# Layer 0 of a four-layer network: the two depthwise convolutions, the norms and the input transposes placed anew in the strip cycle

## The chip, the cores and the metric

The kernel runs on one core of a Trainium2 chip. TensorE (PE) multiplies matrices and transposes, VectorE (DVE) works elementwise and reduces, ScalarE (ACT) evaluates activation functions, GpSimd (POOL) works elementwise, and SyncE (SP) issues most DMAs. Each engine takes its instructions in its own program order and waits on semaphores for the others. The metric is the device time of one execution in microseconds (us); lower is better.

## The reference, cut to what matters

The network has four layers; the change touches layer 0. Its input is eight images of 64 x 64 positions with 192 channels, in fp32. With the shapes left out, layer 0 computes for every image:

```python
def layer0(x):
    x0 = group_norm(x)                      # statistics over a whole image
    x1 = x0 + dwconv3x3(x0, cpe1)           # first depthwise convolution
    h  = layernorm(x1, ln1)
    z, xBC, dt = in_proj(h)                 # 384, 512 and 6 columns
    xBC = silu(causal_conv1d(xBC, 4 taps))
    dt  = softplus(dt + dt_bias)
    y   = ssd(xBC, dt, A) + D * x_part      # chunked scan over the 4096 positions
    y   = rms_norm(y * silu(z)) @ out_proj
    x2  = x1 + y
    x2  = x2 + dwconv3x3(x2, cpe2)          # second depthwise convolution
    h2  = layernorm(x2, ln2)
    x3  = x2 + fc2(gelu(fc1(h2)))           # 192 -> 768 -> 192
    return x + x3                           # and statistics of it for layer 1
```

Layer 1 is a four-directional selective scan; layers 2 and 3 are two further 3x3 depthwise convolutions. They come after layer 0 and are the same in both kernels.

## The kernel before, in words

**Strips and cycles.** Channels lie on partitions as 2 x 96. Each image is cut into 8 strips of 512 positions (8 rows of 64), so there are 64 strips. One turn of the main loop (L700-711) is a cycle; in cycle q every stage of the layer works on its own strip: a strip takes several cycles from its input to its output, and the stages of different strips share a cycle. Inside the cycle the main stage, the scan, works on strip q.

**Who sets the order.** Layer 0 is inside `with every_engine(tc)`: the order of the instructions on PE, DVE, ACT and POOL is exactly the order in which the program emits them. Only SP, the DMA queue, is ordered by a scheduler. The stages are Python generators; each `yield` marks a place where another stage may put instructions. `together(...)` goes round its generators and takes one step of each in turn until all are done; a generator named twice in it makes two steps a round, and one given as `beside` moves on only while the others last. `one_by_one(...)` chains generators. A `yield` more or less therefore moves instructions on all engines.

**The three phases of a cycle**, named by the activation table that ScalarE needs:

- *gelu*: `together(widen(q-3), one_by_one(project_xbc(q), project_out(q-1)), conv1(q+1), residual(q-3))`. `widen` (L643, gelu L647) is fc1. `project_xbc` (L399) makes the columns of xBC and runs the causal convolution on DVE. `project_out` transposes the gated result (L608), multiplies with out_proj (L615) and adds to the strip on DVE (L617). `conv1` is the first depthwise convolution: an affine step on ACT that applies the group norm (L322, two of them), then 16 taps on DVE (L304). `residual` adds on POOL (L661).
- *silu*: `exponents(q, 0, made)`, six ACT operations (L506) that prepare chunk 0, then `together(gates(q), beside=[second])`. `gates` multiplies the z columns (L424), and applies silu to them (L432) and to cv, the output of the causal convolution (L438 the last). `second` is `conv2(q-2)`, the second depthwise convolution. Then `exp_and_ln()` loads ACT's table for exp and ln.
- *chunks*: the strip is scanned in 4 chunks of 128 positions. `front` transposes cv (L524) and copies it out of PSUM on ACT (`xb`, L532), makes the score matrix, applies exp on ACT, prepares xdt, xw and xd on POOL (L538-540), multiplies M on DVE (L541) and issues the next chunk's `exponents`. `back` multiplies with the carried state (L563, L565), updates it on DVE (L571, by the product of L565), and adds the chunk's outputs in one bank (L574, L576); DVE (L585, L586) gates them. Beside them run `narrow(q-3)` (fc2: 12 matmul pairs L677, then L680 on DVE adds the residual, and POOL issues the DMA to x1d), and `norms`, a chain of four: `norm1(q+1)` (layer norm: transposes L344, statistics on DVE, rsqrt and scaling on ACT L357, transposes back L369), `steps(q+1)` (the step sizes: L449 on PE, then exp and ln on ACT, then the cumulative sums L477/478 on PE from dA), `norm2(q-2)` (which waits until `conv2` has emitted its last tap), and `take_in` for the image that comes next (loads x, transposes it at L249, copies it to DRAM in channel order, takes statistics; on the last strip of an image it makes the group norm's scale).

**Buffers that tie the stages.** [...] tp 2 (transposes and out_proj), mm 2 (project_xbc, gates, front, the step sizes), fc 1 (narrow), y 3 (widen, back). In SBUF, x0h and res have two buffers, csb three, xs five. The lines that the change turns on:

```python
def bank(tag):
    return mk(psum, [128, NJ], tag, bufs={"tp": 2, "mm": 2, "fc": 1, "y": 3}[tag])
...
def norm2(q):
    if at(q):
        while ("conv2", q) not in done:
            yield
```

Of the kernel before, what the change touches and what calls it, by code (L numbers as in the profile page):

```python
# [33 lines left out]
def mk(pool, shape, tag, **kw):  # L34
    Names.n += 1
    return pool.tile(shape, F32, tag=tag, name=f"{tag}_{Names.n}", **kw)
# [110 lines left out]
def together(*threads, beside=()):  # L147

    threads = list(threads)
    while threads:  # L150
        for t in list(threads) + list(beside):
            if next(t, threads) is threads and t in threads:
                threads.remove(t)
# [20 lines left out]
def layer0(ctx: ExitStack, tc, a, dr, x, x1, mv1, cst):  # L174
# [62 lines left out]
    def take_in(b, r):  # L237
        if b >= B:
            return
        if r == 0:  # L240
            st0[b] = mk(pool, [CP, CT, NCH, 6], "st0")
        xt = mk(pool, [128, NB, C], "xt", bufs=2)
        nc.sync.dma_start(xt, x[b].rearrange("(g j p) c -> g p j c", p=128, j=NB)[r])
        xc = mk(pool, [CP, CT, NJ], "xc", bufs=2)
        yield
        for ct in range(CT):
            ps = bank("tp")[:CP]
            for j in range(NB):
                nc.tensor.transpose(ps[:, j * 128 : (j + 1) * 128], xt[:, j, ct * CP : (ct + 1) * CP], ident)  # L249
            yield  # L250
            nc.scalar.copy(xc[:, ct, :], ps)
            nc.vector.bn_stats(st0[b][:, ct, r, :], ps)
            yield
        nc.sync.dma_start(x0[b][:, :, r * NJ : (r + 1) * NJ], xc)
        if r < NCH - 1:
            return
        mv, d, q = (mk(pool, s, t) for s, t in (([CP, CT, 2], "mv0"), ([CP, CT], "gd"), ([CP, CT], "gq")))
        gm, sc, nb = (mk(pool, [CP, CT], t, bufs=2) for t in ("gm", "sc0", "nb0"))
        for ct in range(CT):
            nc.vector.bn_aggr(mv[:, ct, :], st0[b][:, ct, :, :])  # L260
        yield
        ps = bank("tp")[:CP, 0:CT]
        nc.tensor.matmul(ps, grp, mv[:, :, 0], start=True, stop=True)
        yield
        nc.vector.tensor_copy(gm, ps)
        nc.vector.tensor_tensor(d, mv[:, :, 0], gm, ALU.subtract)
        nc.vector.tensor_tensor(q, d, d, ALU.mult)
        nc.vector.tensor_tensor(q, q, mv[:, :, 1], ALU.add)
        yield
        ps = bank("tp")[:CP, 0:CT]  # L270
        nc.tensor.matmul(ps, grp, q, start=True, stop=True)
        yield
        nc.vector.tensor_scalar(q, ps, EPS, None, ALU.add)
        rsqrt(nc, pool, q, sc, "gr")
        nc.vector.scalar_tensor_tensor(nb, gm, -1.0, sc, ALU.mult, ALU.mult)
        norm[b] = sc, nb
        yield

    def load_strip(q):

        if not at(q):
            return
        b, r = strips[q]
        t = x0h[q] = mk(pool, [CP, CT, HW], "x0h", bufs=2)
        lo, hi = max(0, r * R - 1), min(H, (r + 1) * R + 1)
        d0 = lo - (r * R - 1)
        nc.sync.dma_start(t[:, :, d0 * W : (d0 + hi - lo) * W], x0[b][:, :, lo * W : hi * W])
# [26 lines left out]
    def conv1(q):  # L314
        if not at(q):
            return
        b, r = strips[q]
        t = x0h.pop(q)
        sc, nb = norm[b]
        lo, hi = (W if r == 0 else 0), (HW - W if r == NCH - 1 else HW)  # L320
        for ct in range(CT):
            nc.scalar.activation(  # L322
                t[:, ct, lo:hi], t[:, ct, lo:hi], AF.Identity, bias=nb[:, ct : ct + 1], scale=sc[:, ct : ct + 1]
            )
        if r == 0:
            nc.gpsimd.memset(t[:, :, 0:W], 0.0)
        if r == NCH - 1:
            nc.gpsimd.memset(t[:, :, HW - W :], 0.0)
        v = xs[q] = mk(pool, [CP, CT, HW], "xs", bufs=5)
        yield  # L330
        yield from conv(t, v[:, :, W : W + NJ], c1w, mid[:, 0, :], c1b)

# [54 lines left out]
    def project_xbc(q):  # L387
        if not at(q):
            return
        raw = mk(pool, [128, 4, 3 + NJ], "raw")  # L390
        cv = cvs[q] = mk(pool, [128, 4, NJ], "cv")
        if strips[q][1] == 0:
            nc.gpsimd.memset(raw[:, :, 0:3], 0.0)
        else:
            nc.gpsimd.tensor_copy(raw[:, :, 0:3], halos.pop(q))
        for o in range(4):
            ps = bank("mm")
            for ct in range(CT):
                nc.tensor.matmul(  # L399
                    ps, w_xbc[:, ct, o * 128 : (o + 1) * 128], hn1[q][:, ct, :], start=ct == 0, stop=ct == CT - 1  # L400
                )
            yield
            nc.scalar.copy(raw[:, o, 3:], ps)  # L403
            yield
            nc.vector.tensor_scalar(
                cv[:, o, :], raw[:, o, 3:], cdw[:, o, 3:4], cdb[:, o : o + 1], ALU.mult, ALU.add
            )
            for k in range(3):
                nc.vector.scalar_tensor_tensor(
                    cv[:, o, :], raw[:, o, k : k + NJ], cdw[:, o, k : k + 1], cv[:, o, :], ALU.mult, ALU.add  # L410
                )
        halos[q + 1] = mk(pool, [128, 4, 3], "halo", bufs=2)
        nc.gpsimd.tensor_copy(halos[q + 1], raw[:, :, NJ : NJ + 3])  # L413
        yield
# [221 lines left out]
    def widen(q):  # L636
        if not at(q):
            return
        ff = ffs[q] = mk(pool, [128, 6, NJ], "ff")
        for o in range(6):  # L640
            ps = bank("y")
            for ct in range(CT):
                nc.tensor.matmul(  # L643
                    ps, f1w[:, ct, o * 128 : (o + 1) * 128], hn2[q][:, ct, :], start=ct == 0, stop=ct == CT - 1
                )
            yield
            nc.scalar.activation(ff[:, o, :], ps, AF.Gelu, bias=f1b[:, o : o + 1])  # L647
        del hn2[q]
        yield

    def load_residual(q):
        if at(q):
            b, r = strips[q]
            ress[q] = mk(pool, [CP, CT, NJ], "res", bufs=2)
            nc.sync.dma_start(ress[q], x0[b][:, :, r * NJ : (r + 1) * NJ])

    def residual(q):
        if at(q):
            x2 = x2s.pop(q)
            for ct in range(CT):  # L660
                nc.gpsimd.tensor_tensor(ress[q][:, ct, :], ress[q][:, ct, :], x2[:, ct, :], ALU.add)  # L661
            yield

    def narrow(q):
        if not at(q):
            return
        b, r = strips[q]
        sl = slice(r * NJ, (r + 1) * NJ)
        ff = ffs.pop(q)
        if r == 0:  # L670
            st1[b] = mk(pool, [CP, CT, NCH, 6], "st1", bufs=2)
        res = ress.pop(q)
        xo = mk(pool, [CP, CT, NJ], "xo")
        for ct in range(CT):
            ps = bank("fc")[:CP]
            for o in range(6):
                nc.tensor.matmul(ps, f2w[:, o, ct * CP : (ct + 1) * CP], ff[:, o, :], start=o == 0, stop=o == 5)  # L677
                if ct > 0 or o > 1:
                    yield
            nc.vector.scalar_tensor_tensor(xo[:, ct, :], ps, f2b[:, ct : ct + 1], res[:, ct, :], ALU.add, ALU.add)  # L680
            nc.vector.bn_stats(st1[b][:, ct, r, :], xo[:, ct, :])
        nc.gpsimd.dma_start(x1[b][:, :, sl], xo)
        if r == NCH - 1:
            for ct in range(CT):
                nc.vector.bn_aggr(mv1[:, b, ct, :], st1[b][:, ct, :, :])
        yield

    def one_by_one(*threads):
        for t in threads:
            yield from t  # L690
# [4 lines left out]
    with every_engine(tc):  # L695
        for r in range(NCH):
            if r == NCH - 1:
                exp_and_ln()
            together(take_in(0, r))
        load_strip(0)  # L700
        for q in range(-1, len(strips) + 3):
            load_strip(q + 2)
            load_residual(q - 2)
            together(
                widen(q - 3), one_by_one(project_xbc(q), project_out(q - 1)), conv1(q + 1), residual(q - 3)
            )
            made, second = {}, conv2(q - 2)
            exponents(q, 0, made)
            together(gates(q), beside=[second])
            exp_and_ln()  # L710
            norms = one_by_one(norm1(q + 1), steps(q + 1), norm2(q - 2), take_in(*divmod(q + NCH + 1, NCH)))
            together(front(q, made), norms, narrow(q - 3), back(q, made), norms, second)


@with_exitstack
# [596 lines left out]
```

## Time and profile before

| | us |
|---|---|
| median of 3 runs (26507.2 to 26526.69) | 26510.6 |
| the profiled execution's own time | 26508.04 |
| its span on the core (mean granted TensorE clock 0.942) | 26506.2 |
| layer 0 in it: from the start to the end of its drain | 5740 |
| undisturbed cycle of layer 0, from one first z silu (L432) to the next | 85.4 |

The first two differ by 2.6 us, so durations from the profile can be set beside the median. Layer 0 takes about a fifth of the span; the other four fifths belong to layers 1 to 3. Cycles are read as the distance of ScalarE's first L432 of a cycle to the next. Most are 85.36 to 85.8; the first are 78.67, 68.48, 95.45 and 91.0, some near image boundaries are 87 to 93, and the last full ones are 88.7.

In the cycle from 2999.90 to 3085.30, the groups with the most work, in calls x mean, are on PE L677 24 x 0.65 us, L643 24 x 0.60 and L399 16 x 0.59; on DVE the taps of the second convolution 16 x 0.88 and of the first 16 x 0.74. A DMA of each kind moves 384 KB a cycle (480 for x0h), and the DMA engines are at most partly busy in every slice. In the page, each digit of a row is a tenth of a fortieth of the span (PEclk: of full clock); in a list by stretches, columns are the stretch, its length, then busy us and instructions of each engine, then the granted clock, the DMA share and GB/s. In a list of waits a line names the engine and its waiting instruction, what released it, and total, number and longest wait in us.

### The profile page before, as it was taken

To read this page: it belongs to the slowest core of one execution; us is meant where nothing else is said; L and a number is where in the kernel's file an instruction comes from. 1 tells how busy PE (TensorE), PEld (TensorE's weight loads), DVE (VectorE), ACT (ScalarE), POOL (GpSimd) and SP (SyncE) were. 2 spreads that over 40 slices of the span, in tenths; PEclk is the share of its full clock that TensorE was granted. 3 is DMA by queue.
4 is the path that set the end of the run, shared out by engine and by line. 5 is a ranking of instruction groups with operands and counts; after the bars stand their busy time and mean duration, and the time that the engine had idled before them with its cause. 6 is when DMAs were issued, how large, how long until landed. Compare 5 with 4: busy or idle time off the path is not lost.

```text
span 26506.2 us, 442347 instructions
## 1 busy us (share of the span) xinstructions
PE 23817.3 (90%) x156160; PEld 18514.6 (70%) x156160; DVE 22196.4 (84%) x25001; ACT 20110.0 (76%) x40019; POOL 17618.6 (66%) x18396
## 2 busy tenths in 40 slices
PE   7888888887799999999999999999999999987766
PEld 4444444444478888888888888888888888863322
DVE  6777777655589999999999999999999999986566
ACT  4555555433379999999999999999999999984322
POOL 2222222210079999999999999999999999972100
PEclk8888888888899999999999999999999999998878
DMA  1111111112233333333333333333333333346411
GB/s 55 42 43 43 42 43 42 34 44 89 90 103 97 94 102 96 95 101 96 96 100 98 94 101 97 96 99 98 95 99 99 95 98 97 96 137 198 126 34 29
DMA packets 1461962, 2275.55 MB, mean 86 GB/s; under 512 B 247181, under 2 KB 773133, under 8 KB 1458202
## 3 DMA queue, kind: packets, MB, share of 16 engines
q1 hardware_dynamic: 1445402, 2196.90, 28.2%
q0 software_dynamic: 14336, 50.34, 0.5%
q8 instruction: 1232, 20.19, 0.3%
q14 instruction: 992, 8.13, 0.1%
HBM read 1811.37 MB, written 435.42 MB: 85 GB/s over the span
## 4 chain that ended last, share of the span: by engine, by line
PE 36%; ACT 29%; DVE 13%; POOL 13%; issue 6%; DMA 2%; POOLq 0%; SPq 0%; DVEq 0%; ACTq 0%
ACT dA L1039 12%; POOL hc L1089 10%; PE pd L1045 6%; ACT sb L1023 6%; PE yt L978 5%; DVE h L1080 5%; ACT bd L1023 4%; PE y L643 3%; PE fc L677 3%; DVE x L71 2%; DVE u L823 2%; PE mm L793 2%; DMA yin<-y 2%; PE pd L1047 2%; PE mm L399 2%
## 5 line engine op out<-in xcount | busy, mean ns | idle before, releaser
L1089 POOL TENSOR_TENSOR hc<-h,bc 128x512 f32<-128x512 f32 x12288 | 15425.9, 1289 | 488.7 <-DVE h L1080 342.0
L1080 DVE TENSOR_TENSOR_SCAN h<-dA,st,pd 128x512 f32<-128x512 f32 x10752 | 12949.9, 1263 | 530.9 <-PE pd L1045 369.4
L1039 ACT ACTIVATE dA<-dl,A_logs 128x512 f32<-128x512 f32 x12288 | 8787.0, 715 | 46.9 <-DVE h L1080 39.6
L978 PE MATMUL yt<-sq,hc 128*128 128x128 f32 x49152 | 7488.5, 275 | 198.8 <-POOL hc L1089 97.3
L1045 PE MATMUL pd<-bd,dut 128*128 128x128 f32 x49152 | 6582.1, 277 | 254.4 <-DVE h L1080 232.1
L1045 PEld LDWEIGHTS pd<-bd,dut 128*128 128x128 f32 x49152 | 5969.2, 192 | 610.3 <-PE yt L978 343.0
L978 PEld LDWEIGHTS yt<-sq,hc 128*128 128x128 f32 x49152 | 5668.1, 141 | 642.1 <-POOL hc L1089 623.3
L1023 ACT ACTIVATE sb<-dut,xt 128x384 f32<-128x384 f32 x8192 | 4763.5, 606 | 1.1 <-DVE dut L964 1.0
L1047 PE MATMUL pd<-sq,sb 128*128 128x128 f32 x24576 | 3739.5, 275 | 9.1 <-DVE h L1080 0.2
L1047 PEld LDWEIGHTS pd<-sq,sb 128*128 128x128 f32 x24576 | 2820.9, 141 | 480.6 <-DVE dl L951 380.8
L1023 ACT ACTIVATE bd<-sq,xt 128x128 f32<-128x128 f32 x8192 | 3011.1, 393 | 0.0
L1080 DVE TENSOR_TENSOR_SCAN h<-dA,pd 128x512 f32<-128x512 f32 x1536 | 1772.6, 1204 | 114.8 <-PE pd L1045 75.6
L71 DVE SCALAR_TENSOR_TENSOR x<-x,w,x 96x3969 f32<-96x3969 f32 (+1 forms) x192 | 838.3, 4366 | 488.6 <-ACT x L64 485.6
L538 POOL TENSOR_TENSOR xdt<-xb,dtv 128x384 f32<-128x384 f32 x256 | 220.7, 862 | 1365.5 <-ACT xb L532 1365.5
L800 POOL COPY xa<-xa 128x192 f32<-128x192 f32 x56 | 19.9, 356 | 1387.9 <-ACT xa L797 1387.9
L413 POOL COPY halo<-raw 128x12 f32<-128x12 f32 x64 | 12.8, 201 | 1380.8 <-ACT raw L403 1380.8
L304 DVE SCALAR_TENSOR_TENSOR x<-xs,cpe_w,x 96x504 f32<-96x504 f32 (+1 forms) x1024 | 899.4, 878 | 30.2 <-ACT x L292 20.4
L823 DVE SCALAR_TENSOR_TENSOR u<-xa,conv_w,u 128x504 f32<-128x504 f32 x1152 | 850.1, 743 | 63.5 <-ACT u L817 25.1
L937 PE MATMUL mm<-xs,w_dt 13*128 13x512 f32 x1536 | 863.0, 641 | 1.8 <-DVE dl L951 1.0
L677 PE MATMUL fc<-ff,fc_w 128*96 128x512 f32 x1536 | 858.9, 676 | 2.7 <-DVE xo L680 2.7
L1091 POOL COPY st<-h 128x3 f32<-128x3 f32 x4096 | 821.8, 201 | 0.0
L793 PE MATMUL mm<-g,w_in 96*128 96x512 f32 x768 | 487.5, 769 | 333.4 <-ACT g L739 332.9
(234 smaller groups left out, 26955.9 us busy)
## 6 DMA issues: line engine op xcount, KB each, us to landing
bc<-bcd SPq DMA_DIRECT2D x4096, 256.0 KB
yin<-y SPq DMA_DIRECT2D x256, 768.0 KB
csb<-csd SPq DMA_DIRECT2D x256, 384.0 KB
dut<-ut SPq DMA_DIRECT2D x128, 768.0 KB
y<-ys SPq DMA_DIRECT2D x128, 768.0 KB
dut<-ut SPq DMA_DIRECT2D x256, 384.0 KB
y<-ys SPq DMA_DIRECT2D x256, 384.0 KB
xt<-x1d SPq DMA_DIRECT2D x128, 384.0 KB
```

The source lines that it names most:

```text
L71: nc.vector.scalar_tensor_tensor(d[:, h0:h1, w0:w1], s[:, h0 + dy : h1 + dy, w0 + dx : w1 + dx], w[:, ct, tap : tap + 1], d[:, h0:h1, w0:w ...
L304: nc.vector.scalar_tensor_tensor(d[:, :, w0:w1], s[:, dy : dy + R, w0 + dx : w1 + dx], w[:, ct, tap : tap + 1], d[:, :, w0:w1], ALU.mult, ...
L677: nc.tensor.matmul(ps, f2w[:, o, ct * CP : (ct + 1) * CP], ff[:, o, :], start=o == 0, stop=o == 5)
L793: nc.tensor.matmul(ps, w_in[:, ct, o * 128 : (o + 1) * 128], g[:, ct, :], start=ct == 0, stop=ct == CT - 1)
L823: nc.vector.scalar_tensor_tensor(uv[:, o, :, w0:w1], tv[:, o, dy : dy + R, w0 + dx : w1 + dx], cw[:, o, tap : tap + 1], uv[:, o, :, w0:w1] ...
L978: nc.tensor.matmul(yt[:, t * 128 : (t + 1) * 128], src[:, t * 128 : (t + 1) * 128], mat, is_transpose=mat is ident, start=first and t == 0 ...
L1023: nc.scalar.activation(v, src, AF.Copy, scale=m["xt"][:, t, 1 + R1 + n : 2 + R1 + n])
L1039: nc.scalar.activation(dA, ready[s]["dl"][:, o, :], AF.Exp, scale=aneg[:, k, o, n : n + 1])
L1045: nc.tensor.matmul(dst, ready[s]["dut"][:, t, cols], brows[g, t], start=True, stop=True)
L1047: nc.tensor.transpose(dst, brows[g, t][:, cols], ident)
L1080: nc.vector.tensor_tensor_scan(h[:, o, rev], decay.pop(j)[:, rev], turned.pop(j)[:, rev], 0.0 if first else st[:, o, n : n + 1], ALU.mult, ...
L1089: nc.gpsimd.tensor_tensor(hc, h[:, o, :], held[g], ALU.mult)
```

## The change

It does five things in layer 0:

- `conv2` moves from the silu and chunk phases of one cycle to the gelu phase of the next, and `conv1` from the gelu phase to the chunk phase. Everything after conv2 (norm2, widen, residual, narrow) is one cycle later for its strip, so the loop has one more turn, and `xs` needs seven buffers instead of five. Before the loop the first strips' conv1 runs on its own.
- `norms` is now norm1, norm2, steps, statistics in this order.
- `take_in` is split: its transposes run beside `gates` in the silu phase; its statistics stay at the end of `norms`.
- `narrow` holds its first step until four pairs instead of three are emitted, and that first step is taken in the silu phase, ahead of the table load.
- `load_strip` and `load_residual` move with their users by one cycle.

```diff
@@ take_in
         nc.sync.dma_start(x0[b][:, :, r * NJ : (r + 1) * NJ], xc)
-        if r < NCH - 1:
+
+    def statistics(b, r):
+
+        if b >= B or r < NCH - 1:
             return
@@ conv1
-        v = xs[q] = mk(pool, [CP, CT, HW], "xs", bufs=5)
+        v = xs[q] = mk(pool, [CP, CT, HW], "xs", bufs=7)
@@ narrow
-                if ct > 0 or o > 1:
+                if ct > 0 or o > 2:
                     yield
@@ main loop
-            together(take_in(0, r))
+            together(one_by_one(take_in(0, r), statistics(0, r)))
+        together(take_in(1, 0))
         load_strip(0)
-        for q in range(-1, len(strips) + 3):
-            load_strip(q + 2)
-            load_residual(q - 2)
+        load_strip(1)
+        together(conv1(0))
+        for q in range(-1, len(strips) + 4):
+            load_strip(q + 3)
+            load_residual(q - 3)
+            nxt = divmod(q + NCH + 2, NCH)
+            second = conv2(q - 3)
             together(
-                widen(q - 3), one_by_one(project_xbc(q), project_out(q - 1)), conv1(q + 1), residual(q - 3)
+                widen(q - 4), one_by_one(project_xbc(q), project_out(q - 1)), residual(q - 4), second
             )
-            made, second = {}, conv2(q - 2)
+            made = {}
             exponents(q, 0, made)
-            together(gates(q), beside=[second])
+            together(gates(q), take_in(*nxt), second)
+            ff = narrow(q - 4)
+            next(ff, None)
             exp_and_ln()
-            norms = one_by_one(norm1(q + 1), steps(q + 1), norm2(q - 2), take_in(*divmod(q + NCH + 1, NCH)))
-            together(front(q, made), norms, narrow(q - 3), back(q, made), norms, second)
+            norms = one_by_one(norm1(q + 1), norm2(q - 3), steps(q + 1), statistics(*nxt))
+            together(front(q, made), norms, ff, back(q, made), norms, conv1(q + 2))
```

## The prediction

> **What bounds the kernel now.** I read the page's busy shares, then one cycle of layer 0 by stretches, what TensorE waited for in it, the granted clock microsecond by microsecond, and the timeline. The change touches layer 0 only, the first 5740 us.
>
> ```profile
> span 26506.2 us, 442347 instructions
> PE 23817.3 (90%) x156160; PEld 18514.6 (70%) x156160; DVE 22196.4 (84%) x25001; ACT 20110.0 (76%) x40019; POOL 17618.6 (66%) x18396
> ...
> PEclk8888888888899999999999999999999999998878
> ```
>
> In layer 0 (the first eight or nine slices) the clock is 8, not 9. One undisturbed cycle, engines in the order PE, PEld, DVE, ACT, POOL, then clock:
>
> ```profile
> 2999.90:3085.30 85.40, 72.62 (x265) 39.45 (x264) 62.28 (x119) 44.90 (x95) 23.61 (x27) 0.88 0.14 43
> ```
>
> TensorE is busy 72.6 of 85.4 us, VectorE 62.3: TensorE bounds the cycle, partly idle and partly at a lowered clock. What it waited for there (total, times, longest):
>
> ```profile
> PE tp L369 <- ACT lrow L357: 6.2, 1, 6.2
> PE mm L524 <- ACT cv L438: 3.2, 1, 3.2
> PE y L565 <- POOL xw L539: 1.1, 1, 1.1
> PE y L574 <- POOL xd L540: 1.1, 1, 1.1
> ```
>
> 6.2 is norm2's chain after the chunks, 3.2 the silu, twice 1.1 the last chunk, held on GpSimd behind the x1d issue. The clock (the third column from the right):
>
> ```profile
> 3043.00:3044.00 1.00, 0.21 (x2) 0.22 (x3) 0.96 (x2) 0.98 (x2) 0.00 (x0) 1.00 0.94 261
> 3044.00:3045.00 1.00, 1.00 (x6) 0.66 (x4) 0.17 (x1) 1.00 (x1) 0.00 (x0) 0.68 0.06 15
> 3045.00:3046.00 1.00, 1.00 (x6) 0.95 (x6) 0.01 (x1) 0.99 (x3) 0.00 (x0) 0.50 0.02 8
> 3048.00:3049.00 1.00, 1.00 (x4) 0.43 (x3) 0.00 (x0) 0.00 (x0) 1.00 (x2) 1.00 0.00 0
> 3078.00:3079.00 1.00, 0.96 (x2) 0.12 (x2) 1.00 (x2) 0.00 (x0) 1.00 (x1) 0.74 1.02 377
> 3094.00:3095.00 1.00, 1.00 (x6) 0.78 (x5) 0.00 (x0) 0.68 (x2) 0.00 (x0) 0.50 0.00 0
> 3096.00:3097.00 1.00, 1.00 (x4) 0.52 (x3) 0.84 (x2) 1.00 (x2) 0.00 (x0) 1.00 0.14 25
> ```
>
> After each hole the clock falls to half: for 3.4 us after the silu, from 3078.5 to 3095.6 around the tail. What half speed costs, same instructions twice:
>
> ```profile
> 3065.52 0.81 PE L574 MATMUL y<-xd,sq 128*128 128x384 f32 x2
> 3066.16 1.45 PE L576 MATMUL y<-xdt,M 128*128 128x64 f32 x12
> ...
> 3080.03 1.65 PE L574 MATMUL y<-xd,sq 128*128 128x384 f32 x2 [1.07 <-POOL xd L540]
> ...
> 3081.47 2.66 PE L576 MATMUL y<-xdt,M 128*128 128x64 f32 x12
> ```
>
> [...] every change of clock in layer 0 lies on one grid of 3.413 us, and the undisturbed cycle is 25 windows. I counted from the matmul records what each window of layer 0 streamed (0.84 ns a column, from 0.43 us for 512 columns in fc; times rows used of 128; over 3413 ns). At full clock all 133 windows up to 0.40 were followed by half clock, all 1041 others, from 0.40 up, kept it. At half clock the clock came back after windows of 0.72 and more; none above 0.78 failed. [...] fc has one bank, and the trace of before shows no long wait on it.
>
> **The change, part by part.** PE times at full clock, from the chain of waits: a pair for fc 0.86, widen or xbc unit 1.72, z unit 1.3; chunk: front 0.96, L563 0.84, L565 0.79, L574+L576 1.93; norm transposes 0.45 each (first group), 0.5 (second).
>
> Removed: the tail wait 6.2, as norm2 moves behind norm1 (its conv2 is now finished in the gelu phase); 2.1 of half clock on L369 and L249 there (2.1+1.94 against half of it); 2.8 of half clock on L565, the last L574/L576 and L344; 2.2 of GpSimd waits, because narrow ends a chunk earlier and the x1d issue with it; the silu hole 3.2, filled by eight transposes and four fc pairs (4 x 0.86 = 3.4; it was three pairs, after the hole), and its half-clock window, 1.7. Sum 18.2; left 85.4 - 18.2 = 67.2. DVE, ACT and POOL work per cycle is unchanged: conv1 and conv2 change places (16 taps each; 744 ns a tap in the gelu phase, 876 beside GpSimd's work in the chunks, by the cycle's groups: with places the durations change over, the sum stays), bn_stats goes to the silu phase. I cost the longer DVE queue at nothing: 62 us fit in the cycle; the input transposes wait for L617's banks, which I find free 0 to 2 us in time; a DVE later than that delays TensorE one for one.
>
> Added, with t=0 at the first z unit and the order of instructions that the changed code gives:
> (1) *fc's single bank.* z, transposes and four pairs end at 9.6, front, norm1 transposes and the last two pairs at 13.3. Next on PE is the first pair of the second half. It needs L680 on VectorE, which now stands behind norm1's statistics, L354 and L541. ACT: silu done 9.0, second xc copy 0.58, table 1.28, exp 0.84, then conv1's two L322 (1.73, newly ahead of the chunk), xb 0.53: 14.0; rsqrt 0.45; DVE five small steps 1.0, L541 0.95, L680 0.75: 17.3. Wait 4.0; behind it stand all of chunk 0's L563 to L576.
> (2) *Its half clock.* A window with 4.0 us idle is under 0.40. Then come fc, L563 (64 rows of 128), L565, front: under 0.72 until the next fc and L574. Back at 26 to 29.6, whatever the phase: 10 us at half, 5.0 lost.
> (3) *L449 behind chunk 3's front.* The step projection now stands there, no longer beside chunk 1, and its mm bank is freed by xb's copy L532. On ACT that follows L587, six L506 (1.85), two hn2 (1.6), exp 0.84 and its own 0.53; all behind L585/L586 of chunk 1, which TensorE ends 4.5 us before it has done front 3. Wait 2.8.
> (4) *L477* waits for dA, now behind L585/L586 of chunk 2: 1.8.
> (5) *Half clock again.* 2.8 idle, L449 (96 columns in 1.7 us) and front are far under 0.40, and no fc is left to lift it: L449 partly 0.6, L574/L576 2.0, L477/478 0.95, L563/L565 1.5, L574/L576 2.0: 7.0. By the phase of the grid it comes back inside the last chunk (1.0 less), or one or two windows into the gelu phase (2.6 more), evenly: +0.8. In before L449 lay between fc pairs at clock 1.00.
> (6) At the gelu phase's start no wait: the table is loaded before the fourth widen unit needs its bank.
> Sum 4.0+5.0+2.8+1.8+7.0+0.8 = 21.4; cycle 67.2+21.4 = 88.6, 3.2 above 85.4. In full cycles (60): +192.
> Outside them: each image's group-norm statistics lengthened its cycle and the next ones by some 10 us together; now most lies beside chunk 3, and I take 7 back, 7 times: -49. Ends: the first cycles lose norm2's tail (-25, one interval of 95 us against 70), conv1 before the loop +5; the drain of 123 us (5617 to 5740) gets one cycle more, but none of its waits of 6 to 8 us: -20, bounds -40 and +25. Together -40. SP's order changes (csb's third fetch ahead of x0h, res last), but each fetch stays most of a cycle ahead of use; xs grows to seven buffers: nothing.
> +192 - 49 - 40 = +103 on the profiled execution's 26508.0, 26611; the median of the runs, 26510.6, is the same within 3 us: 26610. A cycle is read to 3 us either way (200 us).
>
> **Rivals.** *Clock holds* (the other side): the wait of (3) is short, since ACT has hn2 or exp done sooner, and the second fall (5) with its +0.8 does not come: 88.6 - 7.8 = 80.8, 4.6 below 85.4; -4.6 x 60 - 89 = -365: 26143. For it: chunks with fc between them ran at 1.00 from 3048 to 3078. Against it: 4.4 us after the last fc sufficed for the fall at 3078.5. It decides as soon as the cycle is 1.7 us under my sum (103 / 60): at 86.9 the time is that of before. If fc's wait is short as well, (1) and (2) go too: 80.8 - 9.0 = 71.8, -13.6 x 60 - 89 = -905: 25603, a third of this case.
> *Short fall*: (5) costs its least, 4.8 (fall late, return in the last chunk), without the +0.8, and the waits are 0.8 shorter: 88.6 - 2.2 - 0.8 - 0.8 = 84.8; -0.6 x 60 - 89 = -125: 26383.
> *Longer lock*: the cycle settles on 27 windows, 92.2, as the last cycles of before settled on 26 (88.7): +6.8 x 60 - 89 = +319: 26827. A VectorE late for the transposes' banks by 3 to 4 us would look the same.
> That the change does not do what it says is excluded for the tail by the order on PE: norm2's transposes stand before chunk 2's L574.
>
> **How the numbers follow.** Within 0.2% is 53 us, about what can be told from no change. Forecast 0.43 (0.38 slower, 0.05 same), its own range 26500 to 26750; clock holds 0.24, faster; short fall 0.22 (0.16 faster, 0.06 same); longer lock 0.11, slower. Faster 0.40, same 0.11, slower 0.49. The range 26000 to 26800 leaves out the third of the first rival with both waits short (0.08), and somewhat more than half of the last (0.07).
>
> **What would show it.** Right: no wait L369 on L357; a wait of fc on L680 of about 4 us and of L449 on L532 of 2 to 3 a cycle; clock 0.50 for some 10 us after the first and from L449 to the gelu phase; cycles of 88 to 89 us. Wrong: a clock of 1.00 through chunk 3 with cycles near 81, or fc's wait under 1.5 us, which would spare (1) and (2).

## The result, and the profile after

The changed kernel takes 26671.56 us (median of 4 runs, 26659.44 to 26685.02) against 26512.93 us before: a ratio of 1.0059, 95% interval 1.0043 to 1.0074. It is 0.6% slower. The profiled execution took 26685.02 us, of which the span is 26683.2, against 26508.04 and 26506.2 before.

From `statistics` on, the changed kernel's line numbers are three higher than before: fc2's matmuls are L680 (L677 before), the addition on VectorE that frees their PSUM bank is L683 (L680 before), norm's transposes back L372 (L369), the step projection L452 (L449), the cumulative sums L480 (L477), chunk transposes L527 (L524), the addition to the strip L620 (L617).

The page of the changed kernel, its head and the group of fc2's matmuls (busy, mean ns of one, then idle time just before them and what ended it):

```profile
span 26683.2 us, 442321 instructions
PE 24155.8 (91%) x156160; PEld 18705.4 (70%) x156160; DVE 22356.0 (84%) x25001; ACT 20114.8 (75%) x40020; POOL 17625.2 (66%) x18396
...
PEclk7888888888899999999999999999999999998877
...
L680 PE MATMUL fc<-ff,fc_w 128*96 128x512 f32 x1536 | 878.9, 680 | 339.9 <-DVE xo L683 339.9
```

The number of matmuls is the same (156160), but TensorE is busy for 338.5 us longer (24155.8 against 23817.3) in a span that is only 177.0 us longer. So it waits *less* than before, by 161.5 us, and spends more than that again on running slower. The fc group, which had 2.7 us of idle before it in all, now has 339.9: 5.3 us for each of 64 strips.

What TensorE waited for in one cycle of the changed kernel, counted from chunk 0 to the next chunk 0, 2412.02 to 2500.79 us (total, times, longest):

```profile
PE fc L680 <- DVE xo L683: 5.6, 1, 5.6
PE mm L452 <- ACT xb L535: 2.2, 1, 2.2
PE tp L249 <- DVE xs L620: 1.8, 1, 1.8
PE mm L480 <- DVE dA L475: 1.6, 1, 1.6
PE tp L611 <- ACT yc L613: 1.1, 1, 1.1
```

None of the four waits shown for the kernel before is left: norm2's tail (6.2), the silu hole (3.2) and the two on GpSimd (1.1 each) are gone. Of the five above, those on L683, xb and dA are the three of the prediction. The one of L249 on L620 is new as well: 33.6 us in 18 waits over layer 0, where the prediction had found the banks free 0 to 2 us in time. The last was there before, shorter (L608 on L610, 0.4 us each, 66.8 us in all now against 24.6). The clock around the first, by stretches of 1 us (the clock is the third number from the right):

```profile
2414.00:2415.00 1.00, 0.12 (x1) 0.00 (x0) 0.49 (x3) 0.97 (x4) 0.17 (x1) 1.00 0.00 0
2418.00:2419.00 1.00, 0.00 (x0) 0.00 (x0) 1.00 (x3) 0.74 (x2) 0.14 (x1) 0.50 0.00 0
2424.00:2425.00 1.00, 1.00 (x3) 0.26 (x2) 0.08 (x1) 0.00 (x0) 0.00 (x0) 0.50 0.00 0
2432.00:2433.00 1.00, 1.00 (x6) 0.49 (x4) 0.96 (x2) 0.62 (x1) 0.11 (x1) 1.00 0.00 0
2449.00:2450.00 1.00, 1.00 (x4) 0.93 (x5) 0.36 (x2) 0.14 (x1) 1.00 (x2) 0.50 0.05 16
2462.00:2463.00 1.00, 1.00 (x10) 1.00 (x10) 0.03 (x1) 0.00 (x0) 0.00 (x0) 1.00 1.02 390
```

TensorE is idle in the first two rows and fully busy at half clock in the third. The clock is back only by 2432, falls again behind the second hole, and is back by 2462. In this cycle each fall lasts 13.7 us. All 275 clock records in layer 0 of this trace begin on one grid of 3.413 us, to 10 ns; a step of it is called a window here, so each fall is four windows. The first one begins at 2416.99, inside the hole, which ends at 2419.74; 10.9 us of it lie behind the hole. By the clock records the half clock behind the hole is 10.1 us in the mean of 60 cycles.

For all that follows I took, from the clock records and the matmul records of each trace, the mean over cycles 4 to 62 (58 cycles, image boundaries included), split at the end of a cycle's last fc matmul. "Half" is time at half clock, whether TensorE works or not; all in us:

```
                        to the last fc pair     the rest of the cycle   cycle
                        length  half  idle      length  half  idle
before                   37.97   4.77  3.38      49.14  18.24  9.86     87.11
after                    38.43  12.36  5.94      51.65  20.48  4.97     90.08
e1 six first             25.86   1.59  1.82      59.87  23.95  7.22     85.73
e2 steps second          44.38  16.83  7.00      42.30   7.24  3.04     86.68
e3 narrow late           44.41   9.06  6.34      41.10  11.36  3.80     85.51
e4 twelve fillers        39.13   1.18  0.73      51.09  19.13  4.95     90.22
e5 six fillers           36.20   2.65  1.91      49.05  15.07  4.96     85.25
e6 e1 and e2             26.72   1.12  1.79      49.55   9.36  3.36     76.27
e7 e3 and e2             41.75   6.47  4.86      36.45   3.06  2.81     78.20
e8 affine early          38.51  13.30  5.90      53.38  22.66  5.74     91.89
e9 second hole filled    40.58  13.65  7.15      45.11   4.94  1.40     85.69
e10 pairs spread         45.94  14.30  3.75      32.96   0.59  2.12     78.90
e11 half of them spread  39.37  12.85  3.02      43.43  12.39  1.78     82.80
```

(The fc pairs end earlier or later by kernel, so the two lengths are compared between kernels with the same split of work only.) Before to after: idle 13.24 to 10.91, half clock 23.0 to 32.8. A pair of fc took 1.02 us at full clock (2413.10) and 2.02 at half (2419.74); by that I estimate that the extra 9.8 us at half clock cost half of that, 4.9 us; the matmuls' busy time grew by 5.3. Less 2.3 of idle this is +3.0 us a cycle.

### The profile page after: what moved, and what is told of

It reads as the page before. It is cut to its first block, busy times and chain, and to the rows that moved or that the text cites. A ratio compares the mean times of both kernels' runs of the same rounds, so it can differ in the third digit from the quotient of the medians.

```text
span 26683.2 us, 442321 instructions
## 1 busy us (share of the span) xinstructions
PE 24155.8 (91%) x156160; PEld 18705.4 (70%) x156160; DVE 22356.0 (84%) x25001; ACT 20114.8 (75%) x40020; POOL 17625.2 (66%) x18396
## 4 chain that ended last, share of the span: by engine, by line
PE 34%; ACT 30%; DVE 15%; POOL 12%; issue 7%; DMA 2%; POOLq 0%; SPq 0%; DVEq 0%; ACTq 0%
ACT dA L1049 12%; POOL hc L1099 10%; ACT sb L1033 6%; PE pd L1055 6%; PE yt L988 5%; DVE h L1090 5%; ACT bd L1033 4%; DVE x L71 2%; DVE u L833 2%; PE y L646 2%; PE mm L803 2%; PE y L579 2%; DMA yin<-y 2%; PE pd L1057 2%; PE mm L947 2%
## 5 line engine op out<-in xcount | busy, mean ns | idle before, releaser
L680 PE MATMUL fc<-ff,fc_w 128*96 128x512 f32 x1536 | 878.9, 680 | 339.9 <-DVE xo L683 339.9
L599 POOL TENSOR_SCALAR gt<-gt,rms 128x384 f32<-128x384 f32 x256 | 251.8, 998 | 1100.0 <-DVE rms L170 1100.0
L307 DVE SCALAR_TENSOR_TENSOR xs<-x0h,cpe_w,xs 96x504 f32<-96x504 f32 (+1 forms) x1024 | 899.1, 878 | 25.6 <-ACT xs L295 15.9
```

Of the source, the lines that this page charges most:

```text
L307: nc.vector.scalar_tensor_tensor(d[:, :, w0:w1], s[:, dy : dy + R, w0 + dx : w1 + dx], w[:, ct, tap : tap + 1], d[:, :, w0:w1], ALU.mult, ...
```

## The experiments

All are made from the changed kernel (e10 and e11 from e6); times are medians, each beside runs of the kernel before on the same chip (26503 to 26512 us), ratios are to that. Differences from the changed kernel are between chips, and are good to about 10 us.

### The first hole: fc's one bank behind norm1

**e1, six pairs first.** With all six pairs of the first half in the silu phase, L683 stands on VectorE ahead of norm1's statistics.

```diff
-                if ct > 0 or o > 2:
+                if ct > 0 or o > 4:
```

> Edit: all six pairs of fc2's first half are emitted in the silu phase, so that L683 stands on VectorE ahead of norm1's statistics. Theory A (fc's single bank, held behind norm1 on VectorE, and the half clock that its hole brings): the wait of fc on L683, 5.4 us a cycle in the changed kernel, falls under 1 us, of which some 2 us come back as a wait of L372 on norm1's rows; half-clock time per cycle falls from 32.8 us by 6 or more; 26671 - 62 x (3.4 + 3) = 26270, within 26100 to 26400. Rival B (chunk 0 is held by ScalarE and GpSimd anyway, and the wait only moves to L568, L577 or L372): total idle and half-clock time per cycle within 1.5 us of the changed kernel, 26600 to 26740.

26386.48 us, ratio 0.9955 (0.9940 to 0.9969), 285 less than the changed kernel. What TensorE waited for in it, from 400 to 5600 us (59 or so cycles; longest groups):

```profile
PE mm L452 <- ACT xb L535: 182.1, 59, 4.3
PE tp L372 <- ACT lrow L360: 137.0, 170, 2.0
PE mm L480 <- DVE dA L475: 96.9, 59, 1.6
```

The wait on L683 is gone. As expected some of it returns at L372 (2.3 us a cycle), and L452 waits longer (3.1 against 2.1). The first fall is gone too: half clock to the last fc pair is 1.6 us against 12.4. Rival B is out.

**e4 and e5, fillers in the hole.** Does the idle time cost, or the clock after it? Extra matmuls in the hole remove the idle and leave the wait's end where it is.

```diff
+            if ct == 1:
+                keep = bank("y")
+                for _ in range(12):
+                    nc.tensor.matmul(keep, f2w[:, 0, 0:128], ff[:, 5, :], start=True, stop=True)
             ps = bank("fc")[:CP]
```

> Edit: the changed kernel with twelve extra matmuls of 512 columns (about 0.43 us each, 5.2 us) into a spare y bank ahead of the second half's first pair, their product unused: extra work in place of the hole. Theory A (half the price of the hole is the clock that falls after it): the clock stays at 1.00 through chunk 0, half-clock time per cycle falls by 8 to 12 us, the end of the wait stays where it is; 26671 - 62 x 4 to 6 = 26300 to 26420. Rival E (the wait alone costs, or the clock falls for another reason in chunk 0): 26650 to 26750, the added 5.2 us being hidden in the wait.

26710.40 us, ratio 1.0074 (1.0057 to 1.0090): by its time alone the theory failed, and the time lies where rival E had it. The timeline says why; twelve of them show as 24 records and last 10.46 us, not 5.2:

```profile
2415.76 10.46 PE L681 MATMUL y<-ff,fc_w 128*128 128x512 f32 x24
```

I had taken one record for one matmul; an fp32 matmul here shows as two. So the fillers outlast the wait by 4.9 us, while half clock fell by 12.5 us a cycle as expected, and the two nearly cancel (the cycle is 90.2 us against 90.1). e5 has six.

> Edit: as e4 with six extra matmuls in place of twelve. In e4 each took 0.86 us (it shows as two records of 0.43), so twelve lasted 10.3 us, 4.9 beyond the wait, and the cycle, 90.2 us, was as long as that of the changed kernel (90.1) with half-clock time down from 32.8 to 20.3. Six last 5.2 us and fill the wait alone. Theory A (the clock that falls after the hole costs about 5 us a cycle): half-clock time up to the last fc pair 1 to 3 us as in e4, cycle 85 us, 26360 to 26430. Rival E (the wait alone costs): cycle 90, 26650 to 26700.

26364.08 us, ratio 0.9947 (0.9932 to 0.9962): 307 less than the changed kernel, with *more* work in it and L683 where it was (0.4 us a cycle of the wait is left behind the fillers). The cycle is 85.25 us, 4.8 shorter. So the first hole's own 5.6 us cannot be won by this filling, but keeping the clock through it takes a further 4.8 us off the cycle, and rival E is out. The 4.8 is the sum over the whole cycle and not the first fall alone: the half clock in chunks 0 and 1 (a chunk counted from its first transpose L527 to the next one's) goes from 12.4 us to nothing, but that from chunk 3 on goes from 20.5 to 15.1 too, and L249 waits for L620 by 1.5 us a cycle (87.2 us in all) against 0.4.

**e8, affine early.** The prediction counted conv1's two affine steps on ScalarE in the chain to L683.

```diff
             made = {}
+            first = conv1(q + 2)
+            next(first, None)
             exponents(q, 0, made)
...
-            together(front(q, made), norms, ff, back(q, made), norms, conv1(q + 2))
+            together(front(q, made), norms, ff, back(q, made), norms, first)
```

> Edit: the changed kernel with conv1's two affine steps (L325, 1.72 us on ScalarE) issued ahead of chunk 0's exponents, in the gelu phase, instead of ahead of chunk 0's xb. The prediction counted them in the chain to L683 (part 1). If they are in it one for one: fc's wait 5.4 -> 3.5 to 4.0, cycle -2 to -3, 26480 to 26550. If VectorE's own queue sets it (norm1's statistics end at the same time; its small steps run at 0.6 to 0.75 us each beside GpSimd's xdt, xw and xd, against 0.16 without): GpSimd starts 1.6 us earlier, the wait falls by 0.3 to 1.2 us: 26580 to 26670.

26730.82 us, ratio 1.0086 (1.0071 to 1.0101): slower than the changed kernel, outside both expectations. The wait on L683 is as long as before (327.0 us in 57 waits). The edit freed less than it was meant to: since conv1 starts a step further on, its next step on ScalarE (L295, 0.80 us) now stands ahead of xb in place of the 1.72 us, and one of its taps (L307, 0.74 us) ahead of L683 on VectorE. But ScalarE was not what the chain lacked. In e8 it stands idle until VectorE has ended norm1's statistics (L354):

```profile
1343.40 0.20 ACT L165 ACTIVATE lr_r<-lve 128x4 f32<-128x4 f32 x1 [0.97 <-DVE lve L354]
```

In the changed kernel the two come out nearly together: xb ends 0.63 us after the last fc pair and L354 0.43 us after it (medians of 60 cycles), so that a shorter queue on ScalarE alone can gain 0.2 us at most. What follows is VectorE's own queue. In the changed kernel, first VectorE and then GpSimd (start, duration, in us):

```profile
2415.13 0.55 DVE L167 TENSOR_TENSOR lr_t<-lr_r 128x4 f32<-128x4 f32 x1 [0.57 <-ACT lr_r L166]
2415.72 0.16 DVE L168 TENSOR_TENSOR lr_t<-lr_t,lve 128x4 f32<-128x4 f32 x1
2415.91 0.69 DVE L169 TENSOR_SCALAR lr_t<-lr_t 128x4 f32<-128x4 f32 x1
2416.63 0.75 DVE L170 TENSOR_TENSOR lrs<-lr_r,lr_t 128x4 f32<-128x4 f32 x1
2417.41 0.75 DVE L357 SCALAR_TENSOR_TENSOR lnm<-lmv,lrs 128x4 f32<-128x4 f32 x1
```

```profile
2414.83 0.83 POOL L541 TENSOR_TENSOR xdt<-xb,dtv 128x384 f32<-128x384 f32 x1 [9.14 <-ACT xb L535]
2415.74 0.83 POOL L542 TENSOR_TENSOR xw<-xdt,E 128x384 f32<-128x384 f32 x1
2416.53 0.82 POOL L543 TENSOR_TENSOR xd<-xb,D_skip 128x384 f32<-128x384 f32 x1
2417.32 0.82 POOL L570 TENSOR_TENSOR S<-S,E 64x384 f32<-64x384 f32 x1
```

Four of the five steps on 4 elements each end as a GpSimd operation ends; the one of 0.16 us lies in the change from the first to the second. The lengths go the same way in all of layer 0 of this trace: L169, L170 and L357 took 0.69 to 0.76 us in each of the 178 cases in which a GpSimd operation ran beside them for a part of their time, and at most 0.17 in each of the 334 others; L167 took 0.27 to 0.55 us in 64 cases and at most 0.16 in 128; only L168 kept its 0.16 beside GpSimd in most cases (58 of 64). What holds VectorE there is not shown. In e8 the last two steps take 0.16 us each, and they start after GpSimd's fourth operation has ended (1344.99 + 0.82 = 1345.81):

```profile
1345.09 0.76 DVE L169 TENSOR_SCALAR lr_t<-lr_t 128x4 f32<-128x4 f32 x1
1345.88 0.16 DVE L170 TENSOR_TENSOR lrs<-lr_r,lr_t 128x4 f32<-128x4 f32 x1
1346.08 0.16 DVE L357 SCALAR_TENSOR_TENSOR lnm<-lmv,lrs 128x4 f32<-128x4 f32 x1
```

The five steps took 3.0 us (2415.13 to 2418.16); I had counted 1.0. Why the rest of e8's cycle is longer as well is only partly seen: L452 waits 2.9 us, and 17 of its 59 later cycles are 92.16 to 92.20 us long, which is 27 windows, the "longer lock" of the prediction; the others run from 85.3 to 94.6.

### The second hole: the step sizes behind chunk 3's front

**e2, steps second.**

```diff
-            norms = one_by_one(norm1(q + 1), norm2(q - 3), steps(q + 1), statistics(*nxt))
+            norms = one_by_one(norm1(q + 1), steps(q + 1), norm2(q - 3), statistics(*nxt))
```

> Edit: norm1, steps, norm2 again (the old place of the step sizes), all else as changed. Theory A (steps 3 to 5 of the prediction: L452 behind chunk 3's front and L480 after it cause the second fall): both waits (2.1 and 1.6 us a cycle) are gone, fc's wait stays at 5.4; the fall from chunk 3's front is gone unless norm2's rows, now later, bring a new wait of 3 to 4 us at L372. With it: 26450 to 26600; without it 26150 to 26300. Rival C (the second fall comes from the last chunk itself, which has no fc left, as in the kernel before): the half-clock time at the cycle's end stays within 2 us, 26400 to 26500 from the two waits alone.

26450.24 us, ratio 0.9980 (0.9972 to 0.9987). The waits of e2 from 400 to 5600 us:

```profile
PE fc L680 <- DVE xo L683: 333.4, 61, 5.6
PE tp L372 <- ACT lrow L360: 107.3, 118, 1.8
PE tp L249 <- DVE xs L620: 83.8, 50, 2.0
```

L452 and L480 no longer wait, fc does as before, and norm2's rows now hold L372 by 1.8 us a cycle (in two parts). By its time e2 sits at the edge of theory A's first range, but its wait at L372 is half of what that range assumed, and 26450 is in the middle of rival C's range. The clock decides: from chunk 3 on, half clock falls from 20.5 to 7.2 us where rival C had it within 2, so rival C is out; to the last fc pair it is even longer (16.8 us, with L452 now in that part), which takes back a part of the gain.

**e9, the second hole filled.** Two fillers ahead of L452 and two ahead of L480, in the order of the changed kernel:

```diff
+    def fill():
+        keep = bank("fc")
+        for _ in range(2):
+            nc.tensor.matmul(keep, f1w[:, 0, 0:128], f1w[:, 1, 0:NJ], start=True, stop=True)
...
+        fill()
         pdt = bank("mm")
...
+        fill()
         pcs = bank("mm")
```

> Edit: the changed kernel with two extra matmuls of 512 columns (1.7 us) ahead of L452 and two ahead of L480, into the free fc bank, their product unused: they fill the waits of 2.1 and 1.6 us behind chunk 3's front and nothing else. Theory A (part 5 of the prediction: this hole with L452's few columns starts the second fall): half-clock time after the last fc pair falls from 20.5 us a cycle to 12 or less, cycle 85.5 to 87, 26380 to 26480. Rival C (the last two chunks, without an fc pair, fall by themselves, as in the kernel before, where the rest of the cycle has 18.2 us of half clock): 17 us or more stay, cycle 89.5 to 91, 26620 to 26750.

26393.78 us, ratio 0.9953 (0.9937 to 0.9970), 278 less than the changed kernel. Half clock in the rest falls from 20.5 to 4.9 us and that part from 51.65 to 45.11 us, with the same waits filled by 3.4 us of idle work. Part 5 of the prediction stands: the hole starts the fall, not the last chunks. Of the 6.5 us, 2.1 are given back in the first part: the input transposes L249 now wait for L620 by 1.6 us a cycle (92.7 in all, against 20.4), 1.2 more than before the edit, and half clock there is 1.3 us longer.

### Which part of the change costs what

**e3, narrow late; e7, narrow late and steps second.**

```diff
-                if ct > 0 or o > 2:
+                if ct > 0 or o > 1:
...
-            next(ff, None)
```

> Edit: fc2's pairs start in the chunk phase again (first step holds three pairs, none in the silu phase), all else as changed. Theory A (narrow's early start puts the second half's first pair ahead of L683): fc's wait under 1 us a cycle, a silu hole of about 3 us back before L527, and with fc pairs reaching one chunk further a weaker second fall; idle down by 2 to 3 us, half-clock time down by 6 us or more; 26671 - 62 x 4 to 6 = 26300 to 26420. Rival D (norm1 back to back with the new conv1 affine on ScalarE holds chunk 0, whenever fc starts): fc's wait stays over 3 us, or as much idle stands at L566 to L577 of chunk 0; not under 26600.

> Edit: e3 and e2 together: of the change only the places of the convolutions and of the input transposes are left, and the split of take_in. If the waits on L452 and L480 (1.3 and 2.6 us a cycle in e3) go as in e2 and L372's stays near 1 us: 85.5 - 3.9 and up to 2 us of half clock, cycle 80 to 82, 26050 to 26200. Rival F: the fc pairs, later by a chunk, carry the clock through the last chunks in e3 already (11.4 us of half clock in the rest), and norm2's rows come later now and hold L372 by 3 to 4 us: cycle 84 to 86, 26300 to 26420.

e3: 26404.47 us, ratio 0.9962 (0.9947 to 0.9977). fc's wait is gone, and the silu hole is back in its place:

```profile
PE mm L527 <- ACT cv L441: 171.0, 60, 3.2
PE mm L480 <- DVE dA L475: 154.5, 59, 3.0
PE mm L452 <- ACT xb L535: 74.4, 59, 1.3
```

e7: 25958.42 us, ratio 0.9796 (0.9780 to 0.9813), better than expected. Its cycle is 78.2 us where I had 80 to 82. With e2 and the changed kernel this is a square of the two edits:

```
                          norm1, steps, norm2      norm1, norm2, steps
narrow from the chunks    25958 (e7)               26404 (e3)   +446
narrow from the silu      26450 (e2)   +492        26672 (after) +713
```

So the places of the convolutions and of the input transposes, which is what e7 keeps of the change, gain 552 us against 26511 before. The early start of narrow and the late step sizes each cost over 440 us on top of that, and together more than the whole gain.

**e6, six first and steps second.**

> Edit: e1 and e2 together (first half of fc2 in the silu phase, and norm1, steps, norm2). If the two falls are independent, the first part (to the last fc pair) is short of half clock as in e1 (1.6 us) and the rest as in e2 (7.2 us): cycle 81 to 83, 26100 to 26220. Rival F (what keeps the clock up is the number of fc pairs that are left beside the late chunks; e1 spends them early): the rest of the cycle stays at 15 us or more of half clock, cycle 84 to 86, 26300 to 26400.

25860.97 us, ratio 0.9757 (0.9742 to 0.9771): the fastest of all, 2.4% below the kernel before. Neither expectation held: the cycle is 76.3 us. e1 and e2 alone took 4.4 and 3.4 us off the changed kernel's cycle, together 13.8. In each alone some half clock comes back elsewhere: in e1 that from chunk 2 on grows from 20.5 to 23.9 us, in e2 that up to the end of chunk 2 from 12.4 to 16.8. In e6 they are 9.3 and 1.4. The early start of narrow is not bad in itself. What made it bad was that it stopped between the two halves at the point where VectorE was about to be held.

**e10 and e11, the second half's pairs spread out**, one in every second round (e11: the last three only), to lift the clock in e6's late chunks.

```diff
+                if ct > 0:
+                    yield
```

> Edit: e6 with the second half's six fc pairs one every second round instead of every round, so that they reach the last chunks. Theory (the fall that is left in e6, 9.4 us of half clock after the last fc pair, comes from chunks without fc, as rival F had it for e1): half-clock time of the whole cycle from 10.5 to 4 to 7 us, cycle 72 to 75, 25600 to 25780. Rival (the early chunks need the pairs as much, L372's wait on norm1's rows, 3.1 us a cycle in all, grows when they go, and the fall moves there): cycle 76 to 79, 25840 to 26030.

> Edit: e6 with only the last three fc pairs one every second round; the first three stay one a round. In e10 all six were spread and the fall moved into the first chunks (14.3 us of half clock up to the last fc pair against 1.1 in e6), while the rest had 0.6. If a pair in every second round is enough for the late chunks and the first three hold the early ones: half clock of the whole cycle 2 to 6 us, cycle 72 to 75, 25600 to 25780. If three pairs more are needed in either half: cycle 76 to 79, 25850 to 26020, as in e6 or e10.

e10: 25986.99 us, ratio 0.9799 (0.9785 to 0.9814), as the rival had it. Half clock goes from the rest of the cycle (9.4 to 0.6) into the chunks before the last fc pair (1.1 to 14.3). That pair now stands 19 us later, but counted by chunks it is the same: chunks 1 and 2 go from 0.3 us of half clock to 10.4, chunk 3 and what follows from 9.1 to 1.5. e11: 26191.06 us, ratio 0.9877 (0.9861 to 0.9894), outside both: 25.2 us of half clock a cycle, in both parts, with 4.8 us of idle, which is less than the 5.1 of e6. Which window starts its falls I did not settle.

## Why the prediction held, point by point

The direction, the mechanism and the range were right; the size was 159 us where 100 had been predicted (26610 against 26512.93 and 26510.6). That it came so near is in part luck: undisturbed cycles cost 51 us more than forecast and the last image's 23 less.

- **Removed.** The tail wait, the silu hole and GpSimd's waits went as stated. Over layer 0, L369 on L357 goes from 402.1 to 5.9 us, L524 on L438 from 207.0 to 13.4, and L565 and L574 on GpSimd from 138.8 to 7.3. That is 11.3 us a strip; the prediction's 6.2 + 3.2 + 2.2 is 11.6.
- **(1) fc's bank**: there, but 5.6 us (324.0 in 58 waits) and not 4.0. The mis-sized term is "DVE five small steps 1.0": they took 3.0 beside GpSimd. ScalarE's part of the chain was right (xb ends 0.6 us after the last fc pair, 0.7 in the prediction). But VectorE's statistics come out only 0.2 us ahead of it, so nothing is won by moving the two affine steps away (e8). The other steps of the chain took 0.4 us less than the sum had, so the wait is longer by 1.6 us and not by 2.0.
- **(2) its half clock, 5.0**: right. Behind the hole there are 10.1 us of half clock in the mean (8.5 to 11.4), as the prediction had it, so 5.1 lost. That e5's cycle is 4.8 us shorter agrees, but it is the sum of several shifts.
- **(3), (4)**: 2.1 and 1.6 us measured, 2.8 and 1.8 predicted.
- **(5) half clock through the last chunks, 7.0 and 0.8**: e9 took 6.5 us off that part, which agrees; it did not foresee that 2.1 of it would be lost again in the first part.
- **A cycle**: the mean of 58 grew by 2.97, but the prediction's +3.2 is for undisturbed cycles. Of the first seven images, the 38 cycles away from an image boundary grew by 4.55 (85.74 to 90.30 in the mean). There, half clock cost +6.3 of busy time, predicted +6.2 (12.8 added, 6.6 removed); idle fell by 1.8, predicted 3.0 (8.6 added, 11.6 removed). So the failing part is idle time, and most of it is the fc wait of point (1). The prediction's own sign, cycles of 88 to 89 us, fits only 7 of these 38; most are 89.7 to 92.5.
- **Image statistics, -49, and ends, -40**: from cycle 4 to 62 the 38 undisturbed cycles add 173 us (122 at +3.2 each), the 14 at image boundaries 3 (-4 predicted), and the six of the last image give back 4 where +19 had been forecast: there the kernel before had settled at 88.7 us, not at 85.4. Together 172 against 137. The first four cycles give back 24, near to the prediction (-25 and +5). But from cycle 62 to layer 1 the drain costs +19 (283.1 us against 263.8), where -20 had been taken from bounds of -40 to +25. The waits of 6 to 8 us did go, but smaller ones stand in their place, the hole on L683 (11.4 us in 5 waits) and L347 behind conv2's taps (13.2 in 3, at most 4.7); TensorE is idle for 13 us less there and busy for 33 us more, since a part of each strip's work now comes a cycle later (690 matmul records against 626). Layer 1 starts 167.3 us later than before; the last 10 us of the profiled difference lie in layers 1 to 3, whose code is the same, and the changed kernel's own runs spread over 25 us.
- **Rivals.** The clock does not hold by itself, but e5 and e9, which each keep it for one hole, gave 26364 and 26394. "Clock holds", with the second fall away and the first left, had been put at 26143; e9 is that case, and it is 250 us off. Its cycle is 85.7 us and not 80.8: 1.5 because the changed kernel's is 90.1 and not 88.6, 2.1 given back in the first part, and 1.3 because the end of the fall was worth 6.5 and not 7.8.

## What to carry to other kernels

Where TensorE bounds a stage and its clock falls behind a hole, as here, the hole is paid twice; for the first hole the second payment (about 5 us; e5's cycle is 4.8 shorter) was nearly as large as the first (5.6). So look at where the holes stand and what follows them: 4.8 us of idle with 25.2 us of half clock (e11) was 6.5 us a cycle slower than 5.1 with 10.5 (e6). A change made of several moves should be tried in its parts: this one held a gain of 552 us, and two small moves that turned it into a loss of 159.

## What the runs showed that I had not expected

- VectorE operations on four elements (L170, L357) took 0.75 us beside GpSimd in the changed kernel and 0.16 without it in e8. Nothing in their size shows it.
- Two remedies for two holes were worth far more together than alone: 13.8 us a cycle against 4.4 and 3.4.
- The way down from the full clock and the way back have one line in these traces, and not two. Take what the matmuls stream in a window of 3.413 us (columns x 0.84 ns x rows used of 128, each matmul spread evenly over its record), as a share of the window. In layer 0 of the thirteen traces, from the first clock record on, falls from full clock follow windows of up to 0.39, and the clock was kept from 0.36 up; at half clock it came back from 0.37 up and stayed away up to 0.40. Between 0.356 and 0.402 both happen; outside this band none of the 21,111 windows goes the other way. (In before and after alone, 271 falls follow windows of up to 0.378, and 1973 windows from 0.387 up kept the clock; 271 returns follow windows from 0.370 up, and 850 windows of up to 0.391 stayed at half.) The prediction's 0.72 to 0.78 for the way back are the same figure, as a share of what half clock can stream in a window. So here, as the same matmuls take twice as long at half clock (2.02 us a pair of fc against 1.02), TensorE had to work for about twice as long a part of a window to come back as to stay.
